# Layer 0 of a Mamba-then-attention kernel reissued: 1024-token units in the order of a list schedule, against 512-token tiles interleaved by hand

## Chip, core and metric

The kernel runs on one core of a Trainium2 chip. A core has five engines with an instruction queue each, and each queue runs in order: TensorE (PE in the profile, with its weight loads listed apart as PEld), VectorE (DVE), ScalarE (ACT), GpSimd (POOL) and SyncE (SP, which here only issues DMAs). The metric is device microseconds of one execution. Lower is better.

## What is computed

The input is `x` of shape (4, 512, 32, 32): four images (a batch index b), 512 channels, 1024 positions that are read as a sequence of 1024 tokens. Layer 0 is a group normalisation, then a Mamba block, then a residual add; layer 1 is a group normalisation, then a position-attention block with two 3x3 convolutions, then a residual add. Only layer 0 is changed. Cut to what matters:

```python
xn = layernorm(gn(x))                       # per token, 512 channels
xz = xn @ W_in                              # 512 -> 2 x 1024
xm, z = xz[..., :1024], xz[..., 1024:]
xs = silu(causal_conv4(xm) + conv_b)        # 4 taps along the tokens
proj = xs @ W_x                             # 1024 -> 32 + 16 + 16
dt = softplus(proj[..., :32] @ W_dt + b_dt)
Bm, Cm = proj[..., 32:48], proj[..., 48:]
A = -exp(A_log)                             # (1024, 16)
def step(h, inp):                           # over 1024 tokens, h is (4, 1024, 16)
    dt_t, B_t, C_t, x_t = inp
    h = exp(dt_t[..., None] * A) * h + (dt_t * x_t)[..., None] * B_t[:, None, :]
    return h, einsum('bds,bs->bd', h, C_t)
y = (ys + xs * D_param) * silu(z)
x = x + y @ W_out                           # 1024 -> 512, residual
```

The recurrence is the heart: for each of 4 images, 1024 inner channels (8 groups of 128 partitions, index d) and 16 states (index s), one scan over 1024 tokens. That is 512 scans of 128 x 1024 elements, all float32.

## The kernel before

Layer 0 (lines 106 to 374) works on half images: `T = 512` tokens, 8 half images (index i). `phase1(i)` (L170) normalises a half image, runs the input projection `pxm` (L212), the four-tap convolution (L225, L227 on DVE, from an SBUF copy `xm` of the projection) and the parameter projection `pp` (L237), and sends the B and C rows to DRAM. `load_bc(i)` (L246) reads them back, each row broadcast over 128 partitions, as 16 tiles `bc`. `delta(i, d, ...)` (L275) makes `dt` by a softplus of four ACT activations, one DVE and three POOL operations, and `dtx = dt * xs` on POOL (L301).

The recurrence is the inner loop over d and s, one unit per 512 tokens, 1024 units in all:

```python
nc.scalar.activation(da, dt, AF.Exp, scale=a_sb[:, k : k + 1])          # L340, da in PSUM
nc.gpsimd.tensor_mul(dbx, dtx, bc[:, 0, :])                             # L342, SBUF
nc.vector.tensor_tensor_scan(ht, da, dbx, ..., ALU.mult, ALU.add)       # L344, ht in PSUM
if h + 1 < NH: nc.scalar.copy(state[:, k : k + 1], ht[:, T - 1 : T])    # L348
nc.vector.tensor_mul(hc, ht, bc[:, 1, :])                               # L350, PSUM x SBUF
nc.tensor.matmul(py, ident, hc, start=(s == 0), stop=(s == NS - 1))     # L351, sums over s
```

The second half image of each image starts its scans from `state`, the last column of the first half's. The tiles `da` and `ht` lie in PSUM, two buffers each. The sum over s is a float32 matmul with the identity, accumulated in PSUM. `gate` (L305) makes `silu(z)` and `out_proj` (L255) the output projection of the half image before; weights of both projections stay in SBUF. The pieces of `phase1`, `delta` and `out_proj` are generators that the inner loop drains at hand-set values of s, and the framework's scheduler orders the queues from that. After the last `out_proj`, layer 1 starts with its weight transform (first load `raw_b`, L406); layer 1 is the same in both kernels but for the reciprocal root in `group_stats`.

Of the kernel before, what the change touches and what calls it, by code (L numbers as in the profile page):

```python
# [15 lines left out]
P = 128  # L16
# [11 lines left out]
GS = 16  # L28


@with_exitstack
def mamba_then_pab_kernel(
# [35 lines left out]
    make_identity(nc, ident)  # L68
    eps = cpool.tile([P, 1], F32, tag="eps", name="eps")
    nc.vector.memset(eps, 1e-5)  # L70
    one = cpool.tile([P, 1], F32, tag="one", name="one")
    nc.vector.memset(one, 1.0)
# [4 lines left out]
    ]  # L77

    def group_stats(name, chunks, psum, tag):
# [19 lines left out]
        nc.scalar.activation(rstd, pv[:, :n], AF.Sqrt, bias=eps)  # L99
        nc.vector.reciprocal(rstd, rstd)  # L100
        return mean, rstd

# [3 lines left out]
    with ExitStack() as l0:  # L106
        wp = l0.enter_context(tc.tile_pool(name="l0w", bufs=1))
        xp = l0.enter_context(tc.tile_pool(name="l0x", bufs=3))
        sp = l0.enter_context(tc.tile_pool(name="l0s", bufs=2))
        bp = l0.enter_context(tc.tile_pool(name="l0bc", bufs=NS))  # L110
        mmp = l0.enter_context(tc.tile_pool(name="l0mm", bufs=2, space=PSUM))
        yp = l0.enter_context(tc.tile_pool(name="l0y", bufs=2, space=PSUM))
        ap = l0.enter_context(tc.tile_pool(name="l0a", bufs=2, space=PSUM))
        hp = l0.enter_context(tc.tile_pool(name="l0h", bufs=2, space=PSUM))

        xt, stats = {}, {}

        def load_x(i):
            b, h = divmod(i, NH)
            xt[i] = xp.tile([P, NCC, T], F32, tag="xt", name=f"xt_{i}")  # L120
            src = x[b].rearrange("(c p) h w -> p c (h w)", p=P)
            nc.sync.dma_start(xt[i], src[:, :, h * T : (h + 1) * T])

        for i in range(NH):
            load_x(i)
# [16 lines left out]

        nc.scalar.activation(a_sb, a_sb, AF.Exp)
        nc.vector.tensor_scalar_mul(a_sb, a_sb, -1.0)

        win_sb = wp.tile([P, NCC, 2 * DI], F32, tag="win", name="win_sb")
        win_src = w_in.rearrange("(c p) n -> p c n", p=P)
        for q in range(4):
            w = 2 * DI // 4
            nc.scalar.dma_start(  # L150
                win_sb[:, :, q * w : (q + 1) * w], win_src[:, :, q * w : (q + 1) * w]
            )
# [7 lines left out]
        proj = wp.tile([P, T], F32, tag="proj", name="proj")  # L160
        wpr_sb = wp.tile([P, NDC, C], F32, tag="wpr", name="wpr_sb")
        nc.scalar.dma_start(wpr_sb, w_proj.rearrange("(d p) n -> p d n", p=P))


        hist = wp.tile([P, NDC, 3], F32, tag="hist", name="hist")
        state = wp.tile([P, NDC * NS], F32, tag="state", name="state")

        xs, bcd, bct = {}, {}, {}

        def phase1(i):  # L170


            b, h = divmod(i, NH)
            if h == 0:
                chunks = [[xt[i + k][:, c, :] for k in range(NH)] for c in range(NCC)]
                stats[b] = group_stats(f"l0_{b}", chunks, mmp, "mm")
                yield
            mean, rstd = stats[b]
            t = xt[i]
            pmu = mmp.tile([P, T], F32, tag="mm", name=f"pmu_{i}")  # L180
            for c in range(NCC):
                nc.vector.tensor_scalar(
                    t[:, c, :], t[:, c, :], mean[:, c : c + 1], rstd[:, c : c + 1],
                    ALU.subtract, ALU.mult,
                )
                nc.tensor.matmul(pmu, mean_w, t[:, c, :], start=(c == 0), stop=(c == NCC - 1))
            yield
            for c in range(NCC):
                nc.vector.tensor_sub(t[:, c, :], t[:, c, :], pmu)
            yield  # L190
            pvar = mmp.tile([P, T], F32, tag="mm", name=f"pvar_{i}")
            for c in range(NCC):
                sq = sp.tile([P, T], F32, tag="tmp", name=f"sq_{i}_{c}")
                nc.scalar.activation(sq, t[:, c, :], AF.Square)
                nc.tensor.matmul(pvar, mean_w, sq, start=(c == 0), stop=(c == NCC - 1))
            lrs = sp.tile([P, T], F32, tag="lrs", name=f"lrs_{i}", bufs=1)
            nc.scalar.activation(lrs, pvar, AF.Sqrt, bias=eps)
            yield
            nc.vector.reciprocal(lrs, lrs)
            for c in range(NCC):  # L200
                nc.gpsimd.tensor_mul(t[:, c, :], t[:, c, :], lrs)
                yield
                nc.vector.tensor_scalar(  # L203
                    t[:, c, :], t[:, c, :], lnw_sb[:, c : c + 1], lnb_sb[:, c : c + 1],
                    ALU.mult, ALU.add,
                )
            yield "normed"
            xs[i] = []
            for d in range(NDC):
                pxm = mmp.tile([P, T], F32, tag="mm", name=f"pxm_{i}_{d}")  # L210
                for c in range(NCC):
                    nc.tensor.matmul(  # L212
                        pxm, win_sb[:, c, d * P : (d + 1) * P], t[:, c, :],
                        start=(c == 0), stop=(c == NCC - 1),
                    )
                xm = sp.tile([P, T + 3], F32, tag="xm", name=f"xm_{i}_{d}", bufs=1)
                if h == 0:
                    nc.gpsimd.memset(xm[:, 0:3], 0.0)
                else:
                    nc.scalar.copy(xm[:, 0:3], hist[:, d, :])  # L220
                nc.scalar.copy(xm[:, 3:], pxm)
                if h + 1 < NH:
                    nc.scalar.copy(hist[:, d, :], pxm[:, T - 3 :])
                u = sp.tile([P, T], F32, tag="xs", name=f"xs_{i}_{d}", bufs=2 * NDC)
                nc.vector.tensor_scalar_mul(u, xm[:, 0:T], cw_sb[:, 4 * d : 4 * d + 1])  # L225
                for k in range(1, 4):
                    nc.vector.scalar_tensor_tensor(  # L227
                        u, xm[:, k : k + T], cw_sb[:, 4 * d + k : 4 * d + k + 1], u,
                        ALU.mult, ALU.add,
                    )  # L230
                nc.scalar.activation(u, u, AF.Silu, bias=cb_sb[:, d : d + 1])
                xs[i].append(u)
                yield
            pp = mmp.tile([P, T], F32, tag="mm", name=f"pp_{i}")
            p0 = i % 2 * NP
            for d in range(NDC):
                nc.tensor.matmul(  # L237
                    pp[p0 : p0 + NP, :], wx_sb[:, d, :], xs[i][d],
                    start=(d == 0), stop=(d == NDC - 1),
                )  # L240
            nc.scalar.copy(proj[p0 : p0 + NP, :], pp[p0 : p0 + NP, :])
            bcd[i] = dram.tile([2 * NS, T], F32, tag=f"bcd_{i}", name=f"bcd_{i}")
            nc.sync.dma_start(bcd[i], proj[p0 + RK : p0 + NP, :])
            yield

        def load_bc(i):  # L246

            bct[i] = []
            src = bcd[i].rearrange("(j s) t -> s j t", j=2)
            for s in range(NS):  # L250
                t = bp.tile([P, 2, T], F32, tag="bc", name=f"bc_{i}_{s}")
                nc.sync.dma_start(t, src[s].partition_broadcast(P))
                bct[i].append(t)

        def out_proj(i):  # L255

            b, h = divmod(i, NH)
            src = x[b].rearrange("(c p) h w -> p c (h w)", p=P)
            for c in range(NCC):
                res = sp.tile([P, T], F32, tag="res", name=f"res_{i}_{c}", bufs=1)  # L260
                nc.sync.dma_start(res, src[:, c, h * T : (h + 1) * T])
                po = mmp.tile([P, T], F32, tag="mm", name=f"po_{i}_{c}")
                for d in range(NDC):
                    nc.tensor.matmul(  # L264
                        po, wpr_sb[:, d, c * P : (c + 1) * P], xs[i][d],
                        start=(d == 0), stop=(d == NDC - 1),
                    )
                    if d == NDC // 2 - 1:
                        yield
                nc.vector.tensor_add(res, res, po)  # L270
                nc.sync.dma_start(x1[b][h][c * P : (c + 1) * P, :], res)
                yield
            del xs[i]

        def delta(i, d, got):  # L275


            pd = mmp.tile([P, T], F32, tag="mm", name=f"pd_{i}_{d}")
            rows = slice(i % 2 * NP, i % 2 * NP + RK)
            nc.tensor.matmul(  # L280
                pd, wdt_sb[rows, d * P : (d + 1) * P], proj[rows, :], start=True, stop=True
# [34 lines left out]
        def drain(gen, n=None):  # L316
            while n is None or n > 0:
                if next(gen, "end") == "end":
                    return
                n = n if n is None else n - 1  # L320
# [439 lines left out]
```

## Time and profile before

| | us |
|---|---|
| median of 3 runs | 4087.71 (4085.96 to 4087.77) |
| profiled execution, its own time | 4090.25 |
| its span, first to last instruction | 4088.4 |
| layer 0, until the first `raw_b` load issues | 2525.6 |
| layer 1, from there to the end of the span | 1562.8 |

The profiled execution lies 2.5 us above the median of the runs, and 1.9 us of its time lie outside its span. Mean granted TensorE clock of the span: 0.892 of full speed.

| busy in the stretch, us | PE | DVE | ACT | POOL | clock |
|---|---|---|---|---|---|
| 700 to 2400 (1700 us, steady layer 0) | 1361.7 | 1548.9 | 1064.1 | 1234.3 | 0.95 |
| 0 to 94.9 (before the first `dbx`) | 58.4 | 47.1 | 26.3 | 11.8 | 0.93 |
| 2497.2 to 2525.6 (after the last `dbx`) | 20.6 | 6.9 | 0.0 | 1.3 | 0.94 |

Rows of the profile name an instruction by line, engine, operation and tiles (written tile first, buffer numbers left out), with the shape, the count, the busy time, the mean of one in ns, and the idle time of the engine before it with what ended it. A float32 matmul of 512 columns is two PE instructions.

### The profile page before, as it was taken

What the parts mean: (1) busy time and instruction counts of PE and PEld (TensorE: products, weight loads), DVE (VectorE), ACT (ScalarE), POOL (GpSimd) and SP (SyncE); (2) the same over time, 40 slices, a digit from 0 to 9 for tenths busy, and PEclk for the clock granted to TensorE, in tenths of its full rate; (3) what the DMA queues carried; (4) which work ended last, traced back from release to release, by engine and by line L of the source; (5) the groups of instructions that cost most, each with busy time, mean ns of one, the idle gap of its engine ahead of it and who ended that gap; (6) DMA issues with size and microseconds to landing.
All of it is one profiled execution on the core that took longest, in us unless ns stands there. A gap on an engine that the chain in (4) does not pass through costs nothing.

```text
span 4088.4 us, 24690 instructions
## 1 busy us (share of the span) xinstructions
PE 3091.6 (76%) x6440; PEld 1214.0 (30%) x6440; DVE 2964.2 (73%) x3429; ACT 1704.4 (42%) x2771; POOL 2239.1 (55%) x1622
## 2 busy tenths in 40 slices
PE   6776887886887886887887875002987988988988
PEld 2222332322332322332322322000433333333334
DVE  5989999889999889999889996545434534535525
ACT  3675575675575675575676562101101200200200
POOL 1767767767767767768768783666112122221222
PEclk9998999998998998999999998555898898899799
DMA  4003003003003003002002003774626527428436
GB/s 149 36 1 93 18 4 93 21 1 93 17 5 93 21 1 93 16 6 82 18 4 83 21 0 99 235 266 155 236 85 233 204 85 266 173 94 282 151 111 242
DMA packets 165013, 397.36 MB, mean 97 GB/s; under 512 B 13768, under 2 KB 81608, under 8 KB 140296
## 3 DMA queue, kind: packets, MB, share of 16 engines
q1 hardware_dynamic: 150416, 371.82, 27.1%
q10 hardware_dynamic: 14456, 23.96, 1.7%
q8 instruction: 51, 0.84, 0.1%
q14 instruction: 90, 0.74, 0.1%
HBM read 328.11 MB, written 67.63 MB: 97 GB/s over the span
## 4 chain that ended last, share of the span: by engine, by line
PE 28%; DVE 10%; POOL 9%; issue 7%; DMA 3%; ACT 2%; POOLq 0%; DVEq 0%; SPq 0%; ACTq 0%
PE m_b L613 9%; PE m_o L613 8%; PE pat L661 5%; DVE ht L344 3%; PE psc L519 2%; DVE hc L350 2%; PE py L351 2%; POOL dbx L342 2%; DMA x1t<-x 1%; PE po L264 1%; ACT da L340 1%; DVE xs L227 1%; ACT L340 1%; POOL dt L298 0%; POOL u L297 0%
## 5 line engine op out<-in xcount | busy, mean ns | idle before, releaser
L342 POOL TENSOR_TENSOR dbx<-dtx,bc 128x512 f32<-128x512 f32 x1024 | 1323.5, 1307 | 553.3 <-DVE ht L344 538.8
L351 PE MATMUL py<-hc,ident 128*128 128x512 f32 x2048 | 1126.4, 664 | 449.6 <-DVE hc L350 445.0
L340 ACT ACTIVATE da<-dt,a_sb 128x512 f32<-128x512 f32 x1024 | 699.7, 691 | 418.7 <-DVE ht L344 414.7
L351 PEld LDWEIGHTS py<-hc,ident 128*128 128x128 f32 x2048 | 365.5, 200 | 1169.4 <-DVE hc L350 1015.2
L350 DVE TENSOR_TENSOR hc<-ht,bc 128x512 f32<-128x512 f32 x1024 | 666.7, 677 | 49.2 <-ACT state L348 29.1
L344 DVE TENSOR_TENSOR_SCAN ht<-da,state,dbx 128x512 f32<-128x512 f32 x512 | 636.5, 1277 | 46.5 <-POOL dbx L342 24.1
L344 DVE TENSOR_TENSOR_SCAN ht<-da,dbx 128x512 f32<-128x512 f32 x512 | 607.8, 1218 | 65.1 <-POOL dbx L342 30.0
L613 PE MATMUL m_o<-uw_o,v_o 128*128 128x512 f32 x768 | 341.6, 607 | 56.1 <-DVE v_o L600 56.1
L613 PE MATMUL m_b<-uw_b,v_b 128*128 128x512 f32 x768 | 357.6, 624 | 5.7 <-DVE v_b L600 5.7
L264 PE MATMUL po<-xs,wpr_sb 128*128 128x512 f32 x512 | 255.7, 623 | 16.7 <-POOL xs L371 16.7
L308 PE MATMUL pz<-xt,win_sb 128*128 128x512 f32 x512 | 255.3, 613 | 14.2 <-ACT state L348 10.4
L212 PE MATMUL pxm<-xt,win_sb 128*128 128x512 f32 x512 | 248.7, 611 | 11.1 <-DVE xt L203 7.0
L98 PE MATMUL pv_l<-gdev_l,gm_sb 128*128 128x1 f32 (+1 forms) x40 | 10.9, 342 | 309.8 <-DVE gdev_l L96 309.8
L348 ACT COPY state<-ht 128x1 f32<-128x1 f32 x512 | 78.7, 157 | 379.4 <-DVE ht L344 377.6
L340 ACT ACT_TABLE_LOAD x179 | 229.7, 1283 | 3.1
L613 PEld LDWEIGHTS m_o<-uw_o,v_o 128*128 128x128 f32 x768 | 149.0, 195 | 248.4 <-issue 184.8
L661 PE MATMUL pat<-y_b,st 128*128 128x512 f32 x512 | 220.4, 592 | 0.0
L613 PEld LDWEIGHTS m_b<-uw_b,v_b 128*128 128x128 f32 x768 | 149.4, 198 | 210.8 <-issue 199.9
L227 DVE SCALAR_TENSOR_TENSOR xs<-xm,cw_sb,xs 128x512 f32<-128x512 f32 x192 | 176.0, 917 | 1.8
L667 DVE SCALAR_TENSOR_TENSOR xg<-pat,rz,xg 128x512 f32<-128x512 f32 x32 | 24.1, 752 | 195.9 <-PE pat L661 195.9
L621 ACT ACTIVATE e_o<-m_o 128x512 f32<-128x512 f32 x24 | 14.3, 597 | 336.8 <-PE m_o L613 336.8
L264 PEld LDWEIGHTS po<-xs,wpr_sb 128*128 128x128 f32 x512 | 102.2, 201 | 150.1 <-issue 123.4
(208 smaller groups left out, 3540.2 us busy)
## 6 DMA issues: line engine op xcount, KB each, us to landing
uw_b<-u_b SPq DMA_DIRECT2D x96, 1024.0 KB, 4.8
uw_o<-u_o SPq DMA_DIRECT2D x96, 1024.0 KB, 4.8
bc<-bcd SPq DMA_DIRECT2D x128, 512.0 KB, 5.4
u_b<-o_b SPq DMA_DIRECT2D x16, 768.0 KB, 5.3
u_o<-o_o SPq DMA_DIRECT2D x16, 768.0 KB, 3.8
raw_b<-in_w_bottom_dram SPq DMA_DIRECT2D x8, 1152.0 KB, 9.2
raw_o<-in_w_out_dram SPq DMA_DIRECT2D x8, 1152.0 KB, 9.2
xt<-in_x_dram SPq DMA_DIRECT2D x8, 1024.0 KB, 5.3
```

What stands on the lines that cost most here:

```text
L212: nc.tensor.matmul(pxm, win_sb[:, c, d * P : (d + 1) * P], t[:, c, :], start=(c == 0), stop=(c == NCC - 1),)
L227: nc.vector.scalar_tensor_tensor(u, xm[:, k : k + T], cw_sb[:, 4 * d + k : 4 * d + k + 1], u, ALU.mult, ALU.add,)
L264: nc.tensor.matmul(po, wpr_sb[:, d, c * P : (c + 1) * P], xs[i][d], start=(d == 0), stop=(d == NDC - 1),)
L308: nc.tensor.matmul(pz, win_sb[:, c, DI + d * P : DI + (d + 1) * P], xt[i][:, c, :], start=(c == 0), stop=(c == NCC - 1),)
L340: nc.scalar.activation(da, dt, AF.Exp, scale=a_sb[:, k : k + 1])
L342: nc.gpsimd.tensor_mul(dbx, dtx, bc[:, 0, :])
L344: nc.vector.tensor_tensor_scan(ht, da, dbx, 0.0 if h == 0 else state[:, k : k + 1], ALU.mult, ALU.add)
L350: nc.vector.tensor_mul(hc, ht, bc[:, 1, :])
L351: nc.tensor.matmul(py, ident, hc, start=(s == 0), stop=(s == NS - 1))
L519: nc.tensor.matmul(pt, top[:, m * P : (m + 1) * P], center[:, h * T : (h + 1) * T], start=True, stop=True,)
L613: nc.tensor.matmul(m[q], v[:, q, k, c, :], w[:, c, :], start=(c == 0), stop=(c == NCC - 1 and not extra),)
L661: nc.tensor.matmul(pt, st[m][:, 2 * P * j + h : 2 * P * (j + 1) : 2], xb[m // 2][:, m % 2, :], start=(m == 0), stop=(m == NMC - 1),)
```

## The change

Layer 0 is written anew; the arithmetic asked for stays, its grouping changes.

- **Units.** One unit is a whole image's 1024 tokens of one (b, d, s): 512 units. No carried `state`.
- **Order.** Every piece of work is a `Step` with an engine, a duration in us, the tiles it reads and writes, and a priority. `Plan.issue` is a list scheduler that runs while the program is built: it keeps a clock per engine, per tile ring and for DMA, and calls the steps in the order that it finds; the framework's own reordering is off there.
- **In place.** `da`, the scan's result and its product with C are one tile in SBUF (ring `h`, 7 slots). So scan L701 reads `da` from SBUF.
- **dB.** For even s the product with B is made on ACT and PE: `dtx` is transposed once per (b, d) (`dtxt`), ACT multiplies its eight 128 x 128 blocks by the B column (L658), PE transposes them back into PSUM tile `u` (L672), and the scan reads `u`. For odd s POOL multiplies in place in the loaded B tile `bbc` (L687), and the scan reads that from SBUF.
- **C.** The product with C is made on POOL for 12 of 16 s (L713) and on DVE for s = 1, 5, 9, 13 (L708), all operands in SBUF.
- **Sum over s.** Eight PE transposes of 128 x 128 blocks per unit, accumulated in PSUM (L721); ACT copies the sum out and PE transposes it back (L750).
- **Around it.** Softplus is one activation; ln weights are folded into `W_in`, which is rewritten to DRAM as `wind` and read back in pieces; `silu(z)` and the gated y go through DRAM (`szd`, `gd`); the output projection runs per image, its weights loaded in pieces; the convolution reads PSUM; projections are single matmul steps that the schedule places one by one. The reciprocal root is `exp(-0.5 ln(v + eps))`.

Instructions of layer 0 in the changed program: POOL 688 multiplies of 128x1024 (256 L687, 384 L713, 32 `dtx`, 16 norm); DVE 512 scans, 128 products with C, 192 taps, 128 gate operations; ACT 2048 of L658, 512 exponentials, 157 table loads; PE 960 matmuls of 512 columns and 6656 transposes of 128 columns; SP 512 `cbc` and 256 `bbc` loads of 512 KB each.

```diff
+class Plan:
+    ENGINES = ("PE", "DVE", "ACT", "POOL", "SP")
+    HOP, LOAD, SLACK, AHEAD = 0.1, 1.28, 0.3, 20.0
...
+        while left:
...
+                for s in ready[e]:
+                    if s.prio > last:
+                        continue
+                    t = max(clock[e], s.ready)
+                    for b in s.takes:
+                        turn = b.ring not in queues or queues[b.ring][0] is b
+                        t = max(t, min(free[b.ring])) if free[b.ring] and turn else 1e9
...
+            s.fn()
+            if late:
+                t += self.LOAD
+                table = s.table
+            s.done = clock[s.eng] = t + s.us
+            if s.kb:
+                dma = max(dma, s.done) + s.kb / 300
+                s.done = dma + 2.0
...
+        B_ON_ACT = (0, 2, 4, 6, 8, 10, 12, 14)
+        C_ON_DVE = (1, 5, 9, 13)
...
+        slots = {
+            "xt": 1, "xs": 10, "win": 3, "yt": 1, "dt": 2, "dtx": 2, "dtxt": 2, "cbc": 4,
+            "sc": 3, "h": 7, "sz": 1, "bb": 5, "szl": 1, "rs": 1, "wpr": 2, "res": 3,
+        }
+        plan = Plan(
+            {**slots, "mm": 4, "u": 1, "y0": 1, "y1": 1},
+            ("xt", "u", "h", "cbc", "bb", "sc"),
+        )
+        MM, TR = 0.86, 0.115
...
+        def unit(b, d, s, y):
+            c_bc = buf("cbc", [P, L], f"cbc_{name}")
...
+            if s in B_ON_ACT:
+                u = buf("u", [P, L], f"u_{name}")
+                sc = buf("sc", [P, NT, P], f"sc_{name}")
+                da = buf("h", [P, L], f"da_{name}")
...
+                            nc.scalar.activation(
+                                sc()[:, k, :], dtxt()[:, k, :], AF.Copy,
+                                scale=bt()[:, k, s : s + 1],
+                            )
...
+                        nc.tensor.transpose(
+                            u()[:, k * P : (k + 1) * P], sc()[:, k, :], ident
+                        )
...
+                dbx = u
+            else:
+                b_bc = buf("bb", [P, L], f"bbc_{name}")
...
+                dbx = b_bc
+                step(
+                    "POOL", 2.35, lambda: nc.gpsimd.tensor_mul(dbx(), dtx(), b_bc()),
+                    [dtx], [dbx], prio,
+                )
...
+            hc = da
+            on_dve = s in C_ON_DVE
+            ht = da
+            step(
+                "DVE", 2.28,
+                lambda: nc.vector.tensor_tensor_scan(
+                    ht(), da(), dbx(), 0.0, ALU.mult, ALU.add
+                ),
+                [dbx], [ht], prio,
+            )
+            if on_dve:
+                step(
+                    "DVE", 1.22, lambda: nc.vector.tensor_mul(hc(), ht(), c_bc()),
+                    [c_bc], [hc], prio,
+                )
+            else:
+                step(
+                    "POOL", 2.35, lambda: nc.gpsimd.tensor_mul(hc(), ht(), c_bc()),
+                    [c_bc], [hc], prio,
+                )
...
+                        nc.tensor.matmul(
+                            y[h]()[:, k, :], hc()[:, at * P : (at + 1) * P], ident,
+                            start=(s == 0 and k == 0), stop=(s == NS - 1 and k == NK - 1),
+                            is_transpose=True, skip_group_check=True,
+                        )
...
+        def out_proj(b, prio):
...
+                gt = buf("xt", [P, NDC, T], f"gt_{b}_{h}")
...
+        norms(0, -200)
+        for d in range(NDC):
+            conv1(0, d, -100 + d)
+        params(0, -50)
...
+        out_proj(B - 1, B * NDC * NS)
+        with tc.manual_schedule():
+            plan.issue()
```

## The prediction

> **What bounds the kernel now.** I read the page's slices first, then the groups, then the timeline. The slices give the stages:
>
> ```profile
> PE   6776887886887886887887875002987988988988
> DVE  5989999889999889999889996545434534535525
> ...
> POOL 1767767767767767768768783666112122221222
> PEclk9998999998998998999999998555898898899799
> ```
>
> Layer 0 is the first 25 slices: DVE is at 8 or 9 tenths, POOL at 6 to 8. The groups say who waits for whom:
>
> ```profile
> L342 POOL TENSOR_TENSOR dbx<-dtx,bc 128x512 f32<-128x512 f32 x1024 | 1323.5, 1307 | 553.3 <-DVE ht L344 538.8
> ...
> L340 ACT ACTIVATE da<-dt,a_sb 128x512 f32<-128x512 f32 x1024 | 699.7, 691 | 418.7 <-DVE ht L344 414.7
> ...
> L344 DVE TENSOR_TENSOR_SCAN ht<-da,state,dbx 128x512 f32<-128x512 f32 x512 | 636.5, 1277 | 46.5 <-POOL dbx L342 24.1
> ```
>
> POOL and ACT wait for the scan; the scan hardly waits. So layer 0 is DVE's: 1548.9 busy of 1700 us between 700 and 2400, 91%. The timeline gives the pace of a unit pair:
>
> ```profile
> 656.76 2.46 DVE L344 TENSOR_TENSOR_SCAN ht<-da,state,dbx 128x512 f32<-128x512 f32 x2
> 659.12 1.27 DVE L350 TENSOR_TENSOR hc<-ht,bc 128x512 f32<-128x512 f32 x2
> 660.31 2.46 DVE L344 TENSOR_TENSOR_SCAN ht<-da,state,dbx 128x512 f32<-128x512 f32 x2
> ```
>
> Start to start, a scan of 512 takes 1.18 us and a product 0.6. Both read at most one operand from SBUF, the other from PSUM. What happens when a DVE operation reads two from SBUF is in the weight transform (DVE rows, then POOL rows):
>
> ```profile
> 2640.88 0.95 DVE L421 TENSOR_TENSOR t_b<-raw_b,two_b 128x768 f32<-128x768 f32 x1
> ...
> 2643.97 2.55 DVE L422 TENSOR_TENSOR r_b<-t_b,two_b 128x768 f32<-128x768 f32 x1
> 2646.45 2.55 DVE L423 TENSOR_TENSOR r_b<-t_b,two_b 128x768 f32<-128x768 f32 x1
> ```
> ```profile
> 2645.67 2.51 POOL L420 TENSOR_TENSOR r_b<-t_b,raw_b 128x768 f32<-128x768 f32 x1
> 2648.14 2.51 POOL L421 TENSOR_TENSOR t_b<-raw_b,two_b 128x768 f32<-128x768 f32 x1
> ```
>
> Alone the DVE operation takes 0.95 us (0.87 start to start) and POOL's 1.80 (1.76). Together both take 2.5: they take turns. One round is 2.47, so 1.76 + 0.87 less 0.16 that overlaps.
>
> **What leaves.** 1024 units at 1.78 us of DVE, 512 copies of the state on ACT (79 us busy), the long softplus (POOL L293, L297, L298: 247 us busy), and 1024 identity matmuls of two instructions (about 0.86 us each at full clock, 880 in all).
>
> **What comes, engine by engine**, all of layer 0 at start-to-start times:
> - POOL: 688 multiplies of 128x1024. A row of this size in the weight transform starts 2.29 us after the one before (2623.62 to 2625.91). 1576 us.
> - DVE: a scan of 1024 is not in the trace. Two of 512 in a row give 2.36 at most; 1.18 plus 512 elements at about 2.08 ns (1.18 less a start of 0.12) gives 2.25, which I take. 512 x 2.25 = 1152; 128 products x 1.13 (2596.33 to 2597.46) = 145; 192 taps, 128 gate operations and 96 others of 512 at 0.6 = 250; small ones 30. 1577 us, against 1818 for the units alone before.
> - ACT: 2048 of L658. Their cost lies between 0.16 (the 128x1 copy of L348) and 0.31 (L143, 128x128); 0.31 is the same shape: 635. 512 exponentials x 1.135 (L533) = 581; 157 table loads x 1.283 = 201; the rest about 285. 1700 us.
> - PE: 960 matmuls x 0.86 = 826. Transposes: in L685 ten start to end in 1.25 us with a tail of 0.27, so 0.11 each; 6656 x 0.11 = 732. 1558 us at full clock, 1640 at 0.95.
> - DMA: 768 loads of 0.524 MB and some 126 MB around them, 529 MB. The first `bc` loads move 390 GB/s (95 to 110), later ones 305 (385 to 395): 1360 to 1730 us. On SP they wait in order for 4 `cbc` and 5 `bbc` slots, and the gate's and projection's transfers stand in the same queue; at 230 GB/s needed over 2300 us I cost that at nothing. If the loads came later than that, POOL's product with C would wait first.
>
> Five sums near 1600: it would be a large gain if the engines ran beside each other. But 256 odd scans (L701 with `bbc`) and 128 products on DVE (L708) read two SBUF tiles beside a POOL that also reads two. If they take turns as above, each costs POOL its own time less 0.16: 256 x 2.09 + 128 x 0.97 = 535 + 124 = 659 us. Whether a scan does is not in the trace: the bounds are 0 and 535. The nearest rows are the two-operand ones, and L227, a scalar_tensor_tensor on two SBUF tiles, behaves the same (562.00: 0.72 us; the POOL row that starts in it takes 1.69 for 1.27). I take the whole. DVE then waits about 1 us, half a POOL operation, for some 280 of these 384; behind it in its queue stand the next scans, taps and gate, and PE's transposes, ACT's `mm` tiles wait for those. DVE comes to 1577 + 280 = 1860, below POOL's 1576 + 659 = 2235.
>
> The Trainium skill (SBUF — State Buffer, Who interferes with whom) speaks against this change more broadly: any VectorE instruction with two SBUF inputs contends with a GpSimd instruction that reads SBUF, and the second one blocks until the first ends. No row here shows it for a scan; by the rule's full length (2.25 and 1.13) POOL's sum would be 1576 + 576 + 145 = 2297.
>
> **Ahead of and behind the steady stretch.** Before the first `dbx` at 94.9 half an image is made ready; now a whole one must be. x is in by about 19 (as now), statistics and root with two table loads to 25, normalising and centring of two halves with two roots of 4 us to 48, four POOL multiplies to 57, 64 matmuls x 0.86 to 113, last convolution to 118, 16 `pp` matmuls to 132, then proj copy, `bcd` write (1.6) and load (5.4): 140. Of POOL's 688, 5 lie in there. Behind the last product with C: sum out, transposed and gated 6, `gd` written 3.5, `gt` (2 MB) loaded 8, 32 matmuls 27.5, the second `gt` (ring `xt` has one slot) 8, 32 matmuls 27.5, add and store 3, and some 6 while the clock comes back: 90, for 28 before.
>
> **Sum.** Steady: 683 x 2.29 + 659 = 2223 if the pair DVE-POOL never idles. In-order queues leave gaps: DVE, the bound now, reaches 0.91. The ends are 0.91 and 1.00; between them I take 0.96, since the bound here is two engines' joint time and POOL's queue has five B tiles and seven units to choose ahead: 2316. Layer 0: 140 + 2316 + 90 = 2546, for 2525.6. With layer 1 (1562.8; its root adds an Exp and a table load to each of 16 normalisations, hidden by PE but for the first) and 1.9 outside the span: 4110.7 against 4090.25. The median lies 2.5 below its profile: **4108**. At 1.00 it is 4015, at 0.91 4232.
>
> **The clock.** PE now lives half on transposes. In the trace the clock stays full after windows of 3.4 us with PE half busy or more, and halves after emptier ones. One window holds transposes alone, at half clock, and is followed by full clock (the last two columns before DMA: busy PE, then PEclk):
>
> ```profile
> 3123.40:3126.80 3.40, 1.60 (x11) 1.06 (x10) 1.76 (x7) 0.00 (x0) 2.17 (x1) 1.00 0.85 306
> 3126.80:3130.20 3.40, 2.80 (x12) 2.42 (x12) 2.08 (x7) 0.00 (x0) 0.00 (x0) 0.50 0.74 286
> 3130.20:3133.60 3.40, 0.00 (x0) 0.00 (x0) 0.00 (x0) 0.00 (x0) 0.00 (x0) 1.00 0.67 226
> ```
>
> So I count transposes as work: 1558 of 2316 us is 67%, and the clock stays near 0.9. The Trainium skill (TensorE: Matmul & The Clock Gate, Part 4) says that full clock does not engage for transpose mode; by it only the matmuls count, 826 of 2316, PE would stay at half clock with 3116 us, and the whole would come to about 4900.
>
> **Rivals.**
> 1. *The scan does not take turns with POOL* (it takes two cycles or so per element, so it may leave room). Then POOL has 1564 + 124 = 1688, ACT 1650 in the steady stretch, DMA up to 1730: at 0.93 some 1817, layer 0 2047, the whole **3610** (3550 to 3700). Against: every two-SBUF row on DVE. For: no row is a scan. It decides where the turn costs under about 1.5 us per scan instead of 2.09: then layer 0 is over 150 us shorter than forecast. Not slower than before. Chance 0.30.
> 2. *The forecast's mechanism.* 0.65, of which 0.19 under 4079, 0.04 within, 0.42 above.
> 3. *The order stalls*: durations in the plan are those without turns, so the order on each queue fits an even pace that the chip does not keep; below 0.91 of the pair's time, 4240 to 4400. For: `u` has one buffer, and DVE's even scans wait for PE. Against: ACT and PE have 500 us to spare. 0.05.
>
> About 0.2% is what a measurement of this kernel can tell from no change. Faster 0.49, same 0.04, slower 0.47. Likeliest case alone: 4015 to 4232; the range to hold 8 in 10 reaches into rival 1: 3560 to 4220.
>
> **What would show it.** In the profile after: L687 and L713 with a mean over 3 us instead of 2.34; odd scans near 3.2 and even ones (with `u`) at 2.3; the first L687 near 140; layer 1's first load near 2546; L721 with a granted clock of about 0.9. POOL at 2.4 beside odd scans of 2.3 makes rival 1 right; POOL idle for more than a tenth of the steady stretch, rival 3.

## The result, and the profile after

The changed kernel takes 4175.56 us (median of 4 runs, 4171.84 to 4178.99), the kernel before 4086.84 in the same comparison: a ratio of 1.0219 [1.0202, 1.0237]. It is slower by 89 us. The profiled execution took 4174.34 us with a span of 4172.5; the forecast for it was 4110.7. The 64 us between them are taken up again in the part on why the prediction was right or wrong.

The page's slices, to be laid beside those of before:

```profile
PE   7866888787887777877866556001987987988888
...
DVE  3678999877998887998788981554534434525525
...
POOL 0598987987989997889999990476221221221222
PEclk9987899887998888998986768555898898799799
```

In layer 0 POOL is now the fuller of the two: from the third slice to the 24th POOL is at 7 to 9 tenths, mostly 8 or 9, where it was at 6 to 8. DVE is still at 7 to 9, but part of its busy time is now waiting inside instructions. The groups show it (last columns: busy us, mean ns of one, idle before it and what ended that):

```profile
L713 POOL TENSOR_TENSOR da<-da,cbc 128x1024 f32<-128x1024 f32 x384 | 1243.8, 3255 | 178.4 <-DVE da L701 105.6
...
L701 DVE TENSOR_TENSOR_SCAN da<-da,bbc 128x1024 f32<-128x1024 f32 x256 | 812.1, 3177 | 99.4 <-ACT da L693 51.7
...
L687 POOL TENSOR_TENSOR bbc<-dtx,bbc 128x1024 f32<-128x1024 f32 x256 | 784.3, 3074 | 16.2 <-DMA bbc<-bcd 15.7
L701 DVE TENSOR_TENSOR_SCAN da<-da,u 128x1024 f32<-128x1024 f32 x256 | 581.9, 2273 | 171.3 <-PE u L672 115.4
...
L708 DVE TENSOR_TENSOR da<-da,cbc 128x1024 f32<-128x1024 f32 x128 | 327.4, 2558 | 2.5 <-DMA cbc<-bcd 0.5
```

The two rows of L701 are the same instruction on the same shape. With `u` from PSUM it takes 2.27 us, with `bbc` from SBUF 3.18. That the longer one is waiting and not a slower scan can be read from the same trace: 41 of the 256 odd scans start while no POOL instruction is under way, and these take 2.26 to 2.29 us; the other 215 have a mean of 3.35. POOL's multiplies, 2.34 when alone, take 3.1 to 3.3. The timeline shows one such turn being taken (start, duration; POOL's rows, then DVE's):

```profile
1208.67 2.37 POOL L687 TENSOR_TENSOR bbc<-dtx,bbc 128x1024 f32<-128x1024 f32 x1
1211.01 4.33 POOL L687 TENSOR_TENSOR bbc<-dtx,bbc 128x1024 f32<-128x1024 f32 x1
1215.30 4.34 POOL L713 TENSOR_TENSOR da<-da,cbc 128x1024 f32<-128x1024 f32 x1
...
1209.68 3.51 DVE L701 TENSOR_TENSOR_SCAN da<-da,bbc 128x1024 f32<-128x1024 f32 x1
1213.12 4.38 DVE L701 TENSOR_TENSOR_SCAN da<-da,bbc 128x1024 f32<-128x1024 f32 x1
```

The scan that starts at 1209.68 finds a POOL multiply under way until 1211.04 and ends 2.15 us after that, about the 2.25 that the forecast gave a scan, less a short overlap. POOL's next multiply starts at 1211.01, waits for the scan's end at 1213.19 and ends 2.15 us later, and so on. From one POOL multiply to the next it is 4.29 us; the forecast had 2.29 + 2.09 = 4.38 for such a round.

The stages, as windows (length, then busy time of PE, PEld, DVE, ACT and POOL, granted clock, DMA share, GB/s): until the first multiply with B, the steady stretch, the tail, layer 1.

```profile
0.00:156.10 156.10, 126.75 (x356) 69.22 (x357) 59.21 (x127) 51.08 (x69) 12.32 (x12) 0.98 0.33 105
156.10:2508.60 2352.50, 1755.67 (x8260) 1210.47 (x8259) 2022.54 (x1106) 1591.13 (x3111) 2135.20 (x683) 0.85 0.64 218
2508.60:2597.90 89.30, 61.13 (x141) 27.36 (x139) 8.45 (x13) 2.43 (x4) 0.00 (x0) 0.86 0.42 130
2597.90:4172.50 1574.60, 1109.29 (x2456) 488.12 (x2456) 707.47 (x772) 208.76 (x328) 472.32 (x208) 0.80 0.55 188
```

Against the forecast: 156.1 for 140, 2352.5 for 2316, 89.3 for 90, 1574.6 for 1562.8. Three of the four came out longer, by 16, 36 and 12 us.

For the steady stretch one more number is needed, the time in which POOL or a two-SBUF operation of DVE (L701 with `bbc`, L708) was under way. Added up from the timeline's rows it is 2234.6 us, for 2223 in the forecast; below it is called the pair's time. It is 0.950 of the stretch.

### The profile page after: what moved, and what is told of

Same layout as the page of the kernel before. It is cut to its first block, busy times and chain, and to the rows that moved or that the text cites. A ratio compares the mean times of both kernels' runs of the same rounds, so it can differ in the third digit from the quotient of the medians.

```text
span 4172.5 us, 33585 instructions
## 1 busy us (share of the span) xinstructions
PE 3052.8 (73%) x11208; PEld 1795.2 (43%) x11208; DVE 2797.7 (67%) x2018; ACT 1853.4 (44%) x3512; POOL 2619.8 (63%) x902
## 5 line engine op out<-in xcount | busy, mean ns | idle before, releaser
L713 POOL TENSOR_TENSOR da<-da,cbc 128x1024 f32<-128x1024 f32 x384 | 1243.8, 3255 | 178.4 <-DVE da L701 105.6
L721 PE MATMUL y<-ident,da 128*128 128x128 f32 x4096 | 676.9, 327 | 451.5 <-POOL da L713 374.9
L701 DVE TENSOR_TENSOR_SCAN da<-da,bbc 128x1024 f32<-128x1024 f32 x256 | 812.1, 3177 | 99.4 <-ACT da L693 51.7
L721 PEld LDWEIGHTS y<-ident,da 128*128 128x128 f32 x4096 | 584.0, 170 | 623.1 <-POOL da L713 485.5
L687 POOL TENSOR_TENSOR bbc<-dtx,bbc 128x1024 f32<-128x1024 f32 x256 | 784.3, 3074 | 16.2 <-DMA bbc<-bcd 15.7
L701 DVE TENSOR_TENSOR_SCAN da<-da,u 128x1024 f32<-128x1024 f32 x256 | 581.9, 2273 | 171.3 <-PE u L672 115.4
L658 ACT ACTIVATE sc<-dtxt,bt_sb 128x128 f32<-128x128 f32 x2048 | 627.6, 390 | 86.7 <-PE u L672 86.5
L672 PE MATMUL u<-ident,sc 128*128 128x128 f32 x2048 | 333.5, 316 | 105.9 <-DVE da L701 88.3
L693 ACT ACTIVATE da<-dt,a_sb 128x1024 f32<-128x1024 f32 x256 | 292.9, 1144 | 163.0 <-PE y L721 162.0
L672 PEld LDWEIGHTS u<-ident,sc 128*128 128x128 f32 x2048 | 285.9, 165 | 173.9 <-DVE da L701 80.3
L666 ACT ACTIVATE da<-dt,a_sb 128x1024 f32<-128x1024 f32 x256 | 292.8, 1144 | 152.5 <-PE y L721 148.9
L708 DVE TENSOR_TENSOR da<-da,cbc 128x1024 f32<-128x1024 f32 x128 | 327.4, 2558 | 2.5 <-DMA cbc<-bcd 0.5
```

Source lines behind the costliest of these rows:

```text
L658: nc.scalar.activation(sc()[:, k, :], dtxt()[:, k, :], AF.Copy, scale=bt()[:, k, s : s + 1],)
L666: lambda: nc.scalar.activation(da(), dt(), AF.Exp, scale=scale),
L672: nc.tensor.transpose(u()[:, k * P : (k + 1) * P], sc()[:, k, :], ident)
L687: "POOL", 2.35, lambda: nc.gpsimd.tensor_mul(dbx(), dtx(), b_bc()),
L693: lambda: nc.scalar.activation(da(), dt(), AF.Exp, scale=scale),
L701: lambda: nc.vector.tensor_tensor_scan(ht(), da(), dbx(), 0.0, ALU.mult, ALU.add),
```

## The experiments

Theory A: a DVE operation on two SBUF tiles, the scan among them, takes turns with POOL, and the pair DVE-POOL bounds layer 0. Rival B: the scan takes no turns, and something else (POOL's rows by themselves, the order on the queues, the single `u`, the transfers) sets the pace.

| kernel | median us | ratio to before | steady stretch | pair's time |
|---|---|---|---|---|
| changed kernel | 4175.56 | 1.0219 [1.0202, 1.0237] | 2352 | 2235 (0.950) |
| 1 before, `da` in SBUF | 4648.57 | 1.1379 [1.1343, 1.1416] | 2964 | 2814 (0.949) |
| 2 odd `da` in PSUM | 3951.17 | 0.9672 [0.9652, 0.9692] | 2119 | 1722 (0.81) |
| 3 10 of 16 units by ACT and PE | 4101.22 | 1.0043 [1.0031, 1.0056] | 2278 | 1971 (0.865) |
| 4 Sqrt root in layer 1 | 4165.90 | 1.0186 [1.0154, 1.0218] | 2349 | |
| 5 normalisation first | 4172.06 | 1.0227 [1.0212, 1.0242] | 2348 | |
| 6 as 3, order counts turns | 3963.30 | 0.9707 [0.9690, 0.9723] | 2142 | 1971 (0.92) |
| 7 as changed, order counts turns | 4209.61 | 1.0315 [1.0300, 1.0330] | 2388 | 2255 (0.944) |
| 8 as 2, order and buffers | 3880.46 | 0.9510 [0.9496, 0.9525] | 2059 | |
| 9 weights in the schedule | 4160.58 | 1.0184 [1.0167, 1.0202] | 2348 | |
| 10 as 8, weights in the schedule | 3880.80 | 0.9498 [0.9481, 0.9514] | 2082 | |
| 11 all products with C on POOL | 4300.46 | 1.0527 [1.0509, 1.0545] | 2475 | 2411 (0.974) |

The stretches of 2 to 11 run from the first multiply with B to the last product with C, that of 1 to its last scan; the pair's time of 1 is that of POOL and all scans. Each ratio is against runs of the kernel before in the same comparison, whose medians lay between 4080.3 and 4087.0.

**1. The kernel before with its scan on two SBUF tiles.** To find the room, the product is written over `da`, and `lrs` shares the ring of `xm`.

```diff
-        ap = l0.enter_context(tc.tile_pool(name="l0a", bufs=2, space=PSUM))
...
-            lrs = sp.tile([P, T], F32, tag="lrs", name=f"lrs_{i}", bufs=1)
+            lrs = sp.tile([P, T], F32, tag="xm", name=f"lrs_{i}", bufs=1)
...
-                    da = ap.tile([P, T], F32, tag="da", name=f"da_{i}_{k}")
+                    da = sp.tile([P, T], F32, tag="da", name=f"da_{i}_{k}", bufs=3)
...
-                    hc = sp.tile([P, T], F32, tag="hc", name=f"hc_{i}_{k}")
+                    hc = da
```

> The kernel before, with the exponential `da` in an SBUF tile (three buffers, and the product with C written over it) instead of a PSUM tile, so that each of its 1024 scans reads two SBUF operands, as the odd scans of the changed kernel do. Units, order and tiles of 512 stay. Theory A (a scan with two SBUF operands takes turns with POOL): POOL 1.23 us and scan 1.18 us less 0.16 can't lie beside each other, 2.25 us per unit for 1.78, at least 2304 us for the 1024 units beside 250 us of POOL's other work; layer 0 is 150 to 450 us longer, 4240 to 4550 us in all, and the scan's mean is 1.8 us or more instead of 1.28. Rival B (the scan takes no turns; POOL was slow in the changed kernel for another reason, such as its tiles of 1024 or the transfers): within 0.5% of before, scans at 1.28.

Measured: 4648.57, 100 us above even the range of A. From its timeline, DVE's and POOL's rows in order of time:

```profile
708.46 1.73 DVE L343 TENSOR_TENSOR_SCAN ht<-da,state,dbx 128x512 f32<-128x512 f32 x1
710.27 1.26 POOL L341 TENSOR_TENSOR dbx<-dtx,bc 128x512 f32<-128x512 f32 x1 [1.17 <-DVE ht L343]
710.29 0.69 DVE L349 TENSOR_TENSOR da<-ht,bc 128x512 f32<-128x512 f32 x1
710.90 1.72 DVE L343 TENSOR_TENSOR_SCAN ht<-da,state,dbx 128x512 f32<-128x512 f32 x1
```

The unit shown takes 2.44 us (the median of all is 2.52), where the forecast's prices give 2.25: the multiply starts after the scan has ended, and the next scan waits for the multiply's end (its 1.72 us hold 0.5 of waiting). In the groups the scans' mean is 1.65 to 1.71, not quite the 1.8 that was expected. So here too the scan takes turns once both its operands lie in SBUF, in tiles of 512 as of 1024, and the kernel is 14% slower where B allowed 0.5%. B is refuted.

**2. The changed kernel with the odd units' exponential in PSUM.**

```diff
-        mmp = l0.enter_context(tc.tile_pool(name="l0mm", bufs=4, space=PSUM))
+        mmp = l0.enter_context(tc.tile_pool(name="l0mm", bufs=2, space=PSUM))
+        ep = l0.enter_context(tc.tile_pool(name="l0e", bufs=1, space=PSUM))
...
-                da = buf("h", [P, L], f"da_{name}")          # odd s
+                da = buf("e", [P, L], f"e_{name}")
...
-            ht = da
+            ht = da if s in B_ON_ACT else buf("h", [P, L], f"h_{name}")
```

> The changed kernel with one part undone: the exponential of the 256 odd units goes to a PSUM tile (one buffer of two banks, taken from `mm`, which falls from four to two) and the scan writes its states to an SBUF tile, so that the odd scan reads one SBUF operand. Theory A: 256 turns of 2.09 leave the pair DVE-POOL: odd scans near 2.3 us instead of 3.18, L687 near 2.4 instead of 3.07, POOL and turns 1564 + 124 = 1690 in the steady stretch; it becomes 1780 to 1950 us (PE was busy 1756 there and may set the end), 3600 to 3800 in all. Rival B (the odd scan is slow by its own two SBUF reads, POOL by something else): DVE loses 230 us but POOL's multiplies stay at 3.1 us, and the time stays within 1.5% of 4175. If two `mm` tiles are too few, PE's groups wait for ACT, and the gain is smaller with POOL's multiplies at 2.4.

Measured: 3951.17, 224 us less than the changed kernel. Its groups, and the window of its steady stretch:

```profile
L714 POOL TENSOR_TENSOR da<-da,cbc 128x1024 f32<-128x1024 f32 x256 | 625.6, 2445 | 200.0 <-DVE da L702 181.0
L688 POOL TENSOR_TENSOR bbc<-dtx,bbc 128x1024 f32<-128x1024 f32 x256 | 655.8, 2573 | 117.6 <-DMA bbc<-bcd 116.7
L702 DVE TENSOR_TENSOR_SCAN h<-e,bbc 128x1024 f32<-128x1024 f32 x256 | 581.8, 2273 | 155.6 <-POOL bbc L688 98.0
```
```profile
164.70:2283.60 2118.90, 1690.33 (x8261) 1138.63 (x8259) 1673.66 (x1106) 1643.00 (x3153) 1679.15 (x683) 0.89 0.69 242
```

The odd scan is at 2.273 us like the even one (2.275), POOL's multiplies are at 2.4 to 2.6: the scan's turns are gone, as A says and B does not. The 128 products with C on DVE still take theirs (a mean of 1.84 us, 1.19 at the least). But the stretch fell by 234 us and not by the 400 to 570 expected. PE, DVE, ACT and POOL are each busy for 0.78 to 0.80 of it, and the waits are spread: POOL for DVE, DVE for POOL and PE, `bbc` for DMA. With the scan's turns gone no single engine is full. What holds the stretch then, the order on the queues, the buffers or the `mm` tiles that went from four to two, was not tested one by one; run 8 changes order and buffers together and gets 60 us of it.

**3, 6 and 7. Fewer turns, and an order that knows of them.** Run 3 moves 64 units; run 6 adds a common clock to the list schedule for POOL multiplies and two-SBUF operations of DVE (`both`); run 7 is that schedule with the units of the changed kernel.

```diff
-        B_ON_ACT = (0, 2, 4, 6, 8, 10, 12, 14)                 # 3 and 6
+        B_ON_ACT = (0, 2, 3, 4, 6, 8, 10, 11, 12, 14)
...
-                    t = max(clock[e], s.ready)                  # 6 and 7
+                    t = max(clock[e], s.ready, turn_at if s.both else 0.0)
...
             s.done = clock[s.eng] = t + s.us
+            if s.both:
+                turn_at = s.done - 0.16
```

> The changed kernel with s = 3 and 11 added to B_ON_ACT: 64 more units make dB*x on ACT and PE, and their POOL multiply and two-SBUF scan go. Theory A: the pair DVE-POOL loses 64 x (2.29 + 2.09) = 280 us; ACT has 157 us more (1591 to 1750) and PE 58, both still below the pair's 1955; the steady stretch falls by 250 to 290 us, 3885 to 3930 in all. Rival B (the order on the queues, or the single buffer of `u` between ACT, PE and DVE, sets the pace): these units wait for `u` too, and the time is 4150 to 4250.

> The kernel with 10 of 16 units through ACT and PE, whose 64 units less for the pair DVE-POOL brought 75 us instead of 280, with one thing more: the list schedule counts the turns (a POOL multiply and a DVE operation on two SBUF tiles don't lie beside each other but for 0.16 us). If the missing 200 us went into an order that was made for engines that run beside each other, the steady stretch (2278) falls to 2060 to 2170 and the whole to 3880 to 4000. If they went into the one buffer of `u`, the transfers or ACT, the order can't mend it: within 1% of 4101.

> The changed kernel, its own units, with the list schedule counting the turns as in the run beside it. Theory A (the pair DVE-POOL is the bound, 2235 of the 2352 us of its steady stretch): another order can only get at the 117 us in which neither of the two works; within 1% of 4175, 4130 to 4215. Rival 3 (an order made without turns stalls the queues, and the turns only fill the waits): 4060 or less.

Run 3 missed: 74 us less than the changed kernel instead of 250 to 290. The pair's time did fall by 264 us, to 1971, close to the 280 of the prices, but the stretch gave only 74 of it. Run 6 shows where the rest was: the same 1971 us of the pair in 2142 us instead of 2278, and 3963, inside the range of its first case. The groups of 3, then of 6:

```profile
L713 POOL TENSOR_TENSOR da<-da,cbc 128x1024 f32<-128x1024 f32 x384 | 1204.9, 3146 | 368.2 <-DVE da L701 277.9
...
L701 DVE TENSOR_TENSOR_SCAN da<-da,u 128x1024 f32<-128x1024 f32 x320 | 728.5, 2276 | 274.5 <-PE u L672 249.6
```
```profile
L717 POOL TENSOR_TENSOR da<-da,cbc 128x1024 f32<-128x1024 f32 x384 | 1210.3, 3164 | 311.9 <-DVE da L705 175.2
L705 DVE TENSOR_TENSOR_SCAN da<-da,u 128x1024 f32<-128x1024 f32 x320 | 728.8, 2277 | 230.2 <-PE u L676 198.2
```

POOL's wait for the scan falls from 278 to 175 us, DVE's for `u` from 250 to 198. The time in which the pair does no work can be laid beside DVE's rows: in 211 of its 308 us in run 3, and in 132 of 172 in run 6, DVE is at a scan with `u`, and in most of that (190 and 107 us) POOL's next multiply starts as that scan ends. POOL then waits for the scan's result and not for a turn. In the changed kernel itself the same order does not help (7: 4209.61, 34 us longer, the pair at 0.944 of its stretch for 0.950). So rival 3, which needed 4060 or less, does not explain the changed kernel. Counting the turns in the order was worth 138 us in the kernel of run 3, where the pair fills 0.865 of the stretch, and nothing where it fills 0.950; other orders were not tried.

**11. More for POOL.**

```diff
-        C_ON_DVE = (1, 5, 9, 13)
+        C_ON_DVE = ()
```

> The changed kernel with C_ON_DVE empty: the 128 products with C that DVE made go to POOL too. Theory A with the prices of the forecast: each leaves DVE, where it cost POOL a turn of 0.97, and comes to POOL at 2.29, so the pair DVE-POOL grows by 128 x 1.32 = 169 us, over 0.95 to 178; 4320 to 4380 in all. If POOL's rows are long for a reason of its own (3.2 us each, turns or not), they add 128 x 3.2 = 410 us, over 4500. If DVE's time sets the pace, 128 x 1.13 to 2.56 leave it and the kernel is faster, under 4100.

Measured: 4300.46, 125 us more than the changed kernel and 20 under the range of A, far from both other cases. The pair's time grew by 176 us, to 2411 (169 by the prices); the stretch grew by only 123, since the pair now fills 0.974 of it. The prices of the sum hold; the share that the pair fills is what moves.

**4. The root of layer 1.**

```diff
-        rsqrt(rstd, pv[:, :n])
+        nc.scalar.activation(rstd, pv[:, :n], AF.Sqrt, bias=eps)
+        nc.vector.reciprocal(rstd, rstd)
```

> The changed kernel with layer 1's (and only its) group root back to Sqrt and a reciprocal on DVE. If the 12 us that layer 1 is longer than before are the second table load and activation in the chain between two images, the stretch from layer 1's first load falls from 1574.6 to 1562 to 1565, about 4164 in all. If they are something else (the state in which layer 0 leaves the queues), it stays within 3 us.

The window from layer 1's first load in this kernel:

```profile
2602.07:4168.30 1566.23, 1107.67 (x2456) 487.59 (x2456) 712.61 (x788) 174.77 (x288) 471.87 (x208) 0.80 0.54 189
```

1566.2 for 1574.6, just above the expected 1562 to 1565: 8.4 of the 11.8 us are the root in this pair of profiles, about 2 us per image. The remaining 3.4 are no more than profiles of this stretch differ by: it takes 1569.0 to 1575.9 us in the eight with the new root and 1559.5 to 1566.2 in the five with the old one, 11 us apart in the mean. The whole is 9.7 us shorter by the medians, but its four runs lie between 4151 and 4170, so for the whole that is not clear of noise.

**5 and 9. The prelude.** Run 5 issues the first image's normalisation ahead of the weights' preparation; run 9 makes that preparation steps of the schedule, with the scaled weights in tiles of their own.

```diff
+        norms(0, -200)                               # 5: ahead of the wind block
+        with tc.manual_schedule():
+            plan.issue()
...
-                nc.vector.tensor_scalar_mul(ws[c], ws[c], lnw_sb[:, c : c + 1])
+        weights(0, -199)                             # 9: loads, small matmuls, scaling
+        weights(1, -120)                             #    into ring "h", stores as steps
```

> The changed kernel with the first image's normalisation issued ahead of the preparation of the input weights (and the loads of w_x and w_dt ahead of both) instead of behind it; all else as it was. If the 16 us by which the first multiply with B came late (156 instead of 140) are the weights' 128 small matmuls and 8 scalings standing ahead of the normalisation on PE, DVE and ACT, it now comes at 135 to 150 and the whole is 6 to 20 us shorter, 4155 to 4170. If the weights are on the path themselves (the first projection needs them scaled, stored and loaded again), it stays within 4 us of 156 or comes later, and the time within 0.2% of 4175.

> The changed kernel with the first image's preparation of the input weights made part of the list schedule: x is loaded first, the small matmuls of the first half of the weights lie between the normalisation's, those of the second half behind it, and the scaled weights go to tiles of their own, so that the scaling on DVE doesn't wait for those matmuls. With the normalisation first alone, the first projection (73.2) still waited for the weights' way through matmul, scaling, store and load. If the prelude's length is these two chains one behind the other, the first projection now starts at 52 to 62 and the first multiply with B comes at 134 to 146 instead of 156, the whole at 4150 to 4168. If the load of weights and x together (6 MB) holds it, it starts no earlier than 68.

In the changed kernel the normalisation stands behind the weights, whose scaling in place waits for 128 PE instructions `pbx`. From its timeline, DVE's rows, then PE's (in brackets: idle before, and what ended it):

```profile
31.08 2.74 DVE L283 TENSOR_SCALAR win<-win,lnw_sb 128x1024 f32<-128x1024 f32 x4 [11.77 <-PE pbx L278]
...
44.74 2.74 DVE L283 TENSOR_SCALAR win<-win,lnw_sb 128x1024 f32<-128x1024 f32 x4 [10.78 <-PE pbx L278]
...
48.12 0.16 DVE L426 SCALAR_TENSOR_TENSOR gnb_l<-gmean_l,grstd_l 128x4 f32<-128x4 f32 x1
...
19.81 26.16 PE L278 MATMUL pbx<-lnb_sb,win 128*128 128x1 f32 x122
...
73.92 56.95 PE L359 MATMUL pxm<-xt,winc 128*128 128x512 f32 x128 [5.14 <-POOL xt L480]
```

In 5 the roots are done at 43 us instead of 71, and nothing is gained (4172.06; first multiply with B at 157.7). PE's rows say why:

```profile
40.34 22.98 PE L464 MATMUL pbx<-lnb_sb,win 128*128 128x1 f32 x128
...
73.19 17.39 PE L322 MATMUL pxm<-xt,winc 128*128 128x512 f32 x33 [9.87 <-DMA winc<-wind]
```

The first projection now waits for the weights. So the prelude is two chains, normalisation and weights, and whichever goes second ends at 73 to 74. In 9 they lie beside each other (PE's rows, then POOL's):

```profile
54.85 10.92 PE L484 MATMUL pbx<-lnb_sb,win 128*128 128x1 f32 x64
65.63 58.08 PE L335 MATMUL pxm<-xt,winc 128*128 128x512 f32 x128
...
57.76 9.25 POOL L458 TENSOR_TENSOR xt<-xt,rs 128x1024 f32<-128x1024 f32 x4 [56.25 <-ACT rs L205]
```

The projections start at 65.6 and the first multiply with B at 149.7: 6.4 of the 16 us, between the two cases of the expectation. The whole is 15 us shorter by the medians (4160.58), more than the prelude accounts for. The second half's small matmuls, 10.9 us, still stand in front of the projections, but that much could not be won: the first of the four POOL multiplies that make `xt` ends at about 60, the last at 67.

**8 and 10. A version that beats both.** Run 8 is run 2 with the order of run 7, the root of run 4, and other buffers (`C_ON_DVE = (5, 9, 13)`, `dt` 3, `dtx` 1, `dtxt` 3, `bb` 4). Run 10 adds the weights of run 9.

> Meant to beat both: odd units with their exponential in PSUM (3951 us as it was run), a list schedule that counts the remaining turns, three products with C on DVE instead of four (5, 9, 13), three `dt` and three `dtxt` tiles with one `dtx` and four B tiles, and the Sqrt root in layer 1. No engine was busy over 80% of that kernel's steady stretch of 2119 us, so order and buffers hold it; if they do, it falls by 40 to 80 us, and with 8 from the root the whole to 3850 to 3910. If PE's clock or the transfers hold it, it stays at 3930 to 3960.

> The fastest kernel so far (exponential of the odd units in PSUM, order that counts the remaining turns, Sqrt root in layer 1: 3880) with the same preparation of the weights: if the prelude gets 10 to 22 us shorter there too, 3855 to 3875.

Run 8 takes 3880.46 us, 0.951 of before, inside its range; what order, buffers and the three products on DVE each gave was not separated. Run 10 misses its own, at 3880.80: its prelude is 10 us shorter, but its steady stretch is 22 longer. The order is not the reason, since by tile names every queue has the same sequence in both steady stretches. Some 13 of the 22 us come from which executions were profiled, the shortest of run 8 (3876.21) and the longest of run 10 (3889.51). By the medians about 10 us remain that took the prelude's gain back; their cause stays open.

## Why the prediction was right or wrong

**Right: the mechanism and the main term.** The scan takes turns with POOL, at the price that was worked out from two rows of another stage: the pair's time is 2234.6 us for 2223. The signals of the mechanism came: L687 and L713 above 3 us, the odd scans at 3.18 (about 3.2 said) and the even ones at 2.27. Those of the stages and the clock did not: the first L687 came at 156 for 140, layer 1's first load at 2598 for 2546, and L721 had a mean granted clock of 0.78 over its own rows for about 0.9. The rule of the Trainium skill (SBUF — State Buffer, Who interferes with whom) that two SBUF inputs contend with GpSimd is borne out for the scan. At full length without overlap the steady stretch's 683 multiplies would give 2285 (2297 for all 688), 50 us above what was measured.

**The direction was in part luck.** The sum said 21 us slower, the kernel is 89 slower, and the chances were 0.49 for faster against 0.47 for slower. The 64 us that the sum missed are 1.5% of the kernel but three times the change that it forecast; as much on the other side would have turned its sign.

**Wrong: the size, by 64 us.** Three terms of the sum were too small, and each is a step that failed: the steady stretch (2316, measured 2352.5), the prelude (140, measured 156.1) and layer 1's root (nothing, measured 11.8).
- *The share that the pair fills*, 0.96 assumed, 0.950 measured: 118 us of the stretch with neither at work for the 93 assumed, 25 us; the pair's own time adds 12. The longest two of these gaps are 15.0 and 11.9 us, both POOL's multiplies of the next image's normalisation (L480) that stand at the head of its queue and wait for the root on ACT. The remaining 90 us are in some 100 short gaps, over half of them ended by a two-SBUF operation of DVE. In 68 us of them DVE is at an even scan, and in 62 of these POOL's next multiply starts as that scan ends: POOL had nothing to do until the scan's result was there, in spite of the five B tiles and seven units that the prediction gave it to choose from. Run 7 shows that an order that counts the turns does not close these gaps; whether another would is open.
- *The prelude*, 140 forecast, 156.1 measured. The step that failed is "statistics and root with two table loads to 25": the weights' preparation was given no time at all, though its 128 PE instructions and scalings share PE's and DVE's queues with the normalisation. They ended at 48 us, 23 later; the normalisation behind them took 26 us where 32 were allowed, which hid some of it. Runs 5 and 9 show that the weights are a chain of their own to the same matmuls, and that laying both side by side brings back 6.
- *Layer 1's root*, costed at nothing, "hidden by PE but for the first": 11.8 us, of which run 4 gives back 8.4 (11 by the means of all profiles). It was not hidden, at 2 to 3 us for each of the four images.

The tail (90 for 89.3) and the time outside the span (1.9 for 1.8) were right.

**The clock** was said to stay near 0.9; it was 0.85 in the steady stretch. That is far from half, though 6656 of layer 0's some 8750 PE instructions are transposes. Cut at the 3.41 us grid on which the granted clock changes, this trace has 77 windows at half clock in which PE did transposes alone and was busy for 80% or more; after 75 of them the clock was full. So it goes against the rule of the Trainium skill (TensorE: Matmul & The Clock Gate, Part 4) and against the 4900 us that it would have given.

**Rival 1's size was wrong too.** Run 2 is nearly the kernel that it describes, without scan turns, and takes 3951 us, not 3610. The rival divided one engine's sum by 0.93; with four engines between 1643 and 1690 us of busy time, none reached more than 0.80 of the stretch. So no run supports the lower end of the range, 3560: no kernel's median came under 3880.

## What to carry to other kernels

Before moving a scan's or a product's operand from PSUM to SBUF, ask whether POOL reads SBUF at the same time; in these float32 kernels a round of one POOL multiply and one such scan took 4.29 us, close to the sum of both, and one operand left in PSUM was worth 224 us (run 2). The bound resource filled 0.944 to 0.974 of the stretch where it was clearly the fullest; where several engines came within 10% of each other, the fullest reached 0.80 (run 2) and 0.84 (run 8), and not 0.93. Follow each chain of a prelude to the instruction that needs it, and charge small work by the queue that it stands in.

## What was not expected of the hardware

- The turn is waited out inside the DVE or POOL instruction: odd scans last 2.26 to 4.53 us by the profile, where the 41 that found no POOL instruction under way took at most 2.29. A busy share of 0.86 (DVE, 2022.5 of 2352.5) is then no measure of an engine's load.
- A scan of 1024 float32 elements takes 2.27 us whether its second operand comes from PSUM (`u`) or, with `da` in PSUM, from SBUF (run 2: 2275 and 2273 ns).
- A matmul with a single column is not small: 128 PE instructions `pbx` of 128x1 took 23.0 us in one piece in run 5, 0.18 us each.
